# Multi-query attention with a residual: the first two batches' weights transposed by TensorE, and the last output products cut in two

## The chip, the core and the metric

The kernel runs on one core of a Trainium2 chip. A core has a matrix engine (TensorE, PE in the profile), three engines for elementwise work (VectorE, DVE; ScalarE, ACT; GpSimd, POOL), a sync engine (SP) whose queue issues most DMAs here, and 16 DMA engines. The engines run side by side and wait for each other by semaphores; each works through its own list of instructions in the order in which the program names them. PE, ACT and DVE reach PSUM, where products land; all reach SBUF.

The metric is the device time of one execution in microseconds (us). The times before are the median of three runs; one further execution was profiled.

## The reference, cut to what matters

x has 64 batches of 128 tokens with 512 features. There are 16 query heads of 64 and one head for keys and values, with a null key and a null value.

```python
xn = layernorm(x, g_in)
q = (xn @ Wq) * scale                      # 16 heads of 64
k, v = split(xn @ Wkv)                     # one head, null key/value in front
sim = einsum('bhid,bjd->bhij', q, k) + bias
sim = where(causal, -max, sim); sim = where(mask, sim, -max)
attn = softmax(sim)
out = einsum('bhij,bjd->bhid', attn, v)    # -> (b, n, 1024)
return x + layernorm(out @ Wo, g_out)
```

## The kernel before

The order of all instructions is written out by hand in `step(n)`, n from -6 to 62, and a few lines after the loop. Each step serves several batches at different stages: it normalizes and transposes tokens some ten batches ahead, makes the q products of four batches at a time (`product`, a Strassen-like scheme with seven products, whose sums are kept by `keep` and joined by `q_out`), makes scores of batch n + 2, the softmax of batch n + 1, the values of batch n and the output of batches before it. Near the end the distances grow by one: from B3 = 58 on, the softmax runs on `eb` = n + 2 and the scores on `nb` = n + 3. B is 64.

A batch passes these stages:

- **Bias** (POOL): `bias_add` (line 466) writes bias plus mask into the score tile S, `null_copy` (475) adds the null columns. S tiles come from a pool of two (tag "s"), so the bias of a batch has to wait until the tile of the batch two before has been read. One batch, B3 + 1 = 59, has its tile in the room of the transposed tokens (tag "xT").
- **Scores** (PE, line 495), in two halves: half 0 is the queries 0 to 63 against the first 64 keys, half 1 the queries 64 to 127 against all. `scores_add` (DVE, 508) adds them into S, `scores_max` (DVE, 513) takes the row maxima.
- **Exps** (ACT, 522), 8 rows of heads for each half, then `rinv` (DVE, 539) and `scale` (POOL, 543).
- **Transpose of the weights**: `blocks_T` (DVE, 575) transposes S in blocks of 32x32 into sb, and `blocks_move` (601) brings these blocks to their places in aTb with 14 DMAs on the queue of SP. With `take`, half of the 14 are issued by ACT; this is done for the first and the last batch. aTb exists once, from batch 56 on twice.
- **Values** (PE, 610): `values` starts the products of aTb with the values, `values_end` finishes and lets ACT move the result to oT (654). Where it is split, a small copy named done (DVE, 642) stands between the two.
- **Output**. Batches 1 to 58 go in pairs through `out_product` (719), `out_keep`, `out_part`, `pair_stats`, `pair_pow`, `pair_norm` (ACT, 765), `pair_residual` (DVE, 769 and 770). Batches 0 and 59 to 63 are "plain": `out_mm` (669) multiplies the eight chunks of oT with wo, followed by `out_stats` (DVE, 774 to 781, with a small pow on POOL), `residual` (ACT 795, POOL 796) and `store`. The first four chunks of oT come from the first of the two evacuations at line 654, the last four from the second.

PSUM rooms: ps_s (tag "s") holds one score half at a time, ps_w has two rooms, ps_q "a" and "c", ps_y "X" and "Y". Loads of x for the residual (`load_res`, 126) have two rooms, so the load of one batch waits on SP's queue until the residual of two before is done, and what is behind it on that queue waits too.

For the first batches: `blocks_T(0)` comes at the end of step -1 with seven of its DMAs on SP, and the other seven are issued by ACT in step 0, between the keep of a q product and the norm; `blocks_T(1)` comes in step 0 and its 14 DMAs on SP, ahead of `tokens_in(2)` (295), the transposed tokens of the third group of batches.

Of the kernel before, what the change touches and what calls it, by code (L numbers as in the profile page):

```python
# [8 lines left out]
FP = mybir.dt.float32  # L9
# [8 lines left out]
def kernel(  # L18
# [440 lines left out]

    def bias_add(b):  # L460
        g, t = divmod(b, GB)
        if b == B3 + 1:
            S[b] = gp.tile([P, R8, ROW], FP, tag="xT", name=f"s_{b}")
        else:
            S[b] = sp.tile([P, R8, ROW], FP, tag="s", name=f"s_{b}")
        nc.gpsimd.tensor_tensor(  # L466
            S[b][:, :, 1 : ROW - 1],
            biasp,
            mneg[g][:, t].unsqueeze(1).broadcast_to([P, R8, NL + N]),
            ALU.add,  # L470
        )
# [109 lines left out]
    def blocks_move(b, take=None):  # L581
# [3 lines left out]
        for u in range(2):  # L585
            for i in range(2):
                src = slice((2 * u + i) * Q, (2 * u + i + 1) * Q)
                for j in range(3 + i):
# [14 lines left out]
                        in_=sb[src, js].rearrange("p s e q -> p s (e q)"),  # L603
                    )

    pos = {}

    def value_mm(b, u, half, keys, vals, slots, start=True):
# [51 lines left out]
                bias=nv2,  # L660
            )

    def out_mm(b):
        pool, tag = ps_w, "w"
        if b > P_LAST:
            pool, tag = (ps_q, "c") if b == P_LAST + 2 else (ps_y, "XY"[b % 2])
        py = pool.tile([P, DIM], FP, tag=tag, name=f"py_{b}")
        for c in range(NC):
            nc.tensor.matmul(  # L669
                py, oT[b][:, c, :], wo[:, c, :], start=(c == 0), stop=(c == NC - 1)  # L670
            )
        ys[b] = py


    HE = DIM // 2
# [79 lines left out]
    def pair_pow(b):  # L755
        nc.gpsimd.tensor_tensor(yn[b][1], yn[b][1], nhalf, ALU.pow)

    def pair_norm(b):
        mv, rstd = yn.pop(b)
        nmr = small.tile([P, 1], FP, tag="nmro", name=f"nmro_{b}")  # L760
        nc.vector.tensor_scalar(nmr, mv[:, 0:1], rstd, -1.0, ALU.mult, ALU.mult)  # L761


        yn[b] = ps_y.tile([P, DIM], FP, tag="Y", name=f"yn_{b}")
        nc.scalar.activation(yn[b], ys[b], AF.Identity, bias=nmr, scale=rstd)
# [74 lines left out]
    def step(n):  # L840
        def ok(b, end=B):
            return 0 <= b < end
# [28 lines left out]
        if second:  # L871
            if n != B3 + 1:
                out_sums(p5673)
        elif ok(nb) and n >= 0:
            bias_add(nb)
            null_copy(nb)
        if third:
# [16 lines left out]
        if third:  # L894
            out_product(p4, 4, ps_y, "X", start=False)
        if one:
            out_mm(n - 1)
            if n == 1:
                out_stats(0)
        if fast:  # L900
            if f == 0:
                q_tile(qg)
            if n % 2:
                product(qg, f, 2, ps_w, "w")
        if last:
            product(last_g, last_f, 4, ps_q, "a", start=False)
        if soft:
# [144 lines left out]
        if n == B3:  # L1052
            out_sums(p12)
            scores(nb, 0)
            scores_add(nb, 0)
            pair_norm(p4 + 1)
            pair_residual(p4 + 1)
            store(p4 + 1)
            scores_max(nb, 0)
# [6 lines left out]
                scores_max(nb, 1)  # L1066
        if ok(n) and split:
            values_end(n, split)
        if eb == B - 1:
            blocks_move(eb, take=0)  # L1070
            blocks_move(eb, take=1)
# [43 lines left out]
        if ok(mk) and not ok(mkv):  # L1115
            kT_out(mk, k_T(mk))
        if n == -1:
            blocks_T(0)
            blocks_move(0, take=0)
        if n == B3 - 2:  # L1120
            bias_add(B3 + 1)
            null_copy(B3 + 1)
            scores(B3 + 1, 0)
            scores_add(B3 + 1, 0)
            scores_max(B3 + 1, 0)
        if 0 <= n < 4:
            out_weight_sum(n)
        if n == B2 - 2:
# [106 lines left out]
```

## Time and profile before

| what | before |
|---|---|
| time, median of 3 runs (lowest to highest) | 1135.81 us (1134.92 to 1136.13) |
| profiled execution, its time | 1134.49 us |
| its span, first to last instruction | 1132.7 us |
| mean granted TensorE clock | 0.995 |
| DMA, mean | 116 GB/s |

The span is what the profile shows; the execution's own time is 1.8 us longer. In timelines each row begins with its start and its length in us, both from the span's start, followed by engine, line, operation, output and inputs, the shapes, the count, and in brackets the idle time of the engine before it with the instruction that ended it. Matmuls of fp32 appear as two records each. Steps can be found in the timeline by their lines: step 0 is near 79 to 99 us, step 1 near 99 to 120; step 57 begins near 1030, step 58 near 1048, step 59 near 1063, step 60 near 1076, step 61 near 1090.

### The profile page before, as it was taken

The numbers are of one execution on the slowest core, as the hardware profiler recorded it, in microseconds if no ns is written. First come the engines' busy times: TensorE is split into PE (matmuls) and PEld (weight loads), VectorE is DVE, ScalarE is ACT, GpSimd is POOL, SyncE is SP. The second block draws the span as 40 slices with busy tenths as digits, with TensorE's granted clock in tenths as the row PEclk, the third lists the DMA queues.
The fourth block names the chain that finished last, engine by engine and source line by source line (L and its number), as shares of the span: only waits on it lengthen the run. The fifth ranks groups of instructions, "written<-read, shape, count | busy, mean of one in ns | idle before, by whom it ended". The sixth has DMA issues, their size and how long they took to land.

```text
span 1132.7 us, 27381 instructions
## 1 busy us (share of the span) xinstructions
PE 1084.5 (96%) x9700; PEld 869.1 (77%) x9700; DVE 807.5 (71%) x1737; ACT 678.5 (60%) x2710; POOL 745.9 (66%) x588
## 2 busy tenths in 40 slices
PE   6877999999999999999999999999999999999897
PEld 4454788888878888888888888888888888887642
DVE  6563677776787777788777778877777886666762
ACT  2344656566756656675666667666666755657661
POOL 5444877767665676857577686757767675676742
PEclk9998999999999999999999999999999999999999
DMA  6314234353453435335353533534353353422333
GB/s 184 123 37 126 73 123 118 93 167 100 126 127 120 115 98 163 103 125 135 104 135 97 164 106 122 136 116 121 97 164 107 120 136 112 103 73 72 95 97 107
DMA packets 109591, 131.39 MB, mean 116 GB/s; under 512 B 29712, under 2 KB 74256, under 8 KB 107664
## 3 DMA queue, kind: packets, MB, share of 16 engines
q1 hardware_dynamic: 107776, 127.95, 40.3%
q10 hardware_dynamic: 1680, 1.71, 0.5%
q8 instruction: 77, 1.26, 0.5%
q14 instruction: 58, 0.48, 0.1%
HBM read 54.86 MB, written 31.46 MB: 76 GB/s over the span
## 4 chain that ended last, share of the span: by engine, by line
PE 71%; POOL 7%; DVE 6%; DMA 6%; SPq 4%; issue 2%; ACT 2%; ACTq 1%; POOLq 0%; DVEq 0%
PE pa L422 15%; PE pyX L719 14%; PE pc L422 7%; PE ps L495 7%; PE pyY L719 7%; PE po L610 7%; PE pk L308 4%; PE pw L422 4%; PE pyw L719 3%; DMA x<-in_x_dram 3%; SPq L601 3%; PE py L669 2%; POOL s L466 2%; POOL xS L404 1%; POOL s L543 1%
## 5 line engine op out<-in xcount | busy, mean ns | idle before, releaser
L522 ACT ACTIVATE s<-s,nmax 128x65 f32<-128x65 f32 (+1 forms) x1024 | 372.1, 368 | 1.3 <-DVE nmax L513 0.9
L466 POOL TENSOR_TENSOR s<-biasp,mneg 128x1536 f32<-128x1536 f32 x64 | 221.1, 3455 | 108.3 <-DVE sb L575 105.1
L543 POOL TENSOR_TENSOR s<-s,rinv 128x512 f32<-128x512 f32 (+1 forms) x128 | 189.4, 1481 | 125.7 <-DVE nmro L761 88.6
L654 ACT ACTIVATE oT<-po,nv 128x512 f32<-128x512 f32 x128 | 81.1, 684 | 210.9 <-PE po L610 210.9
L522 ACT ACTIVATION_READ_ACCUMULATOR s<-s,nmax 128x1 f32 x1024 | 194.7, 190 | 0.0
L719 PE MATMUL pyX<-wT,oT 128*128 128x256 f32 x696 | 164.6, 379 | 1.1 <-DVE kyu L731 1.1
L719 PEld LDWEIGHTS pyX<-wT,oT 128*128 128x128 f32 x696 | 132.0, 190 | 19.8 <-DVE kyu L731 1.5
L508 DVE TENSOR_TENSOR s<-ps,s 128x512 f32<-128x512 f32 (+1 forms) x128 | 121.4, 949 | 14.8 <-PE ps L495 12.7
L495 PEld LDWEIGHTS ps<-kT,qT 64*64 64x64 f32 x4096 | 93.9, 135 | 46.9 <-DVE s L508 24.5
L422 PE MATMUL pa<-xS,wq 128*128 128x256 f32 x480 | 123.6, 380 | 2.5 <-ACT ku L433 1.5
L513 DVE TENSOR_REDUCE nmax<-s 128x8 f32<-128x520 f32 (+1 forms) x128 | 120.1, 938 | 5.1 <-POOL s L475 3.7
L575 DVE STREAM_TRANSPOSE sb<-s 128x1536 f32<-128x1536 f32 x64 | 113.5, 1773 | 11.8 <-POOL s L543 4.9
L495 PE MATMUL ps<-kT,qT 64*64 64x64 f32 (+1 forms) x4096 | 118.4, 252 | 3.7 <-DVE s L508 2.5
L610 PE MATMUL po<-aTb,vs 64*64 64x256 f32 (+1 forms) x1240 | 116.7, 383 | 1.3 <-DMA aTb<-sb 1.3
L433 ACT COPY ku<-pa 128x256 f32<-128x256 f32 x120 | 44.8, 373 | 93.1 <-PE pa L422 93.1
L422 PEld LDWEIGHTS pa<-xS,wq 128*128 128x128 f32 x480 | 86.8, 190 | 13.1 <-ACT ku L433 2.5
L422 PE MATMUL pc<-xS,wS 128*128 128x256 f32 x240 | 63.3, 386 | 8.3 <-POOL xS L404 7.3
L308 PE MATMUL pk<-wkv,xT 128*128 128x144 f32 x488 | 69.9, 286 | 0.0
L443 DVE TENSOR_TENSOR qT<-pw,kp 128x256 f32<-128x256 f32 x60 | 25.4, 423 | 59.9 <-ACT kp L433 59.8
L422 PE MATMUL pa<-xS,wS 128*128 128x256 f32 x240 | 68.0, 406 | 0.0
L610 PEld LDWEIGHTS po<-aTb,vs 64*64 64x64 f32 (+1 forms) x1240 | 57.5, 135 | 10.9 <-issue 4.6
L308 PEld LDWEIGHTS pk<-wkv,xT 128*128 128x128 f32 x488 | 63.4, 191 | 0.2
(114 smaller groups left out, 2060.7 us busy)
## 6 DMA issues: line engine op xcount, KB each, us to landing
aTb<-sb SPq DMA_DIRECT2D x378, 64.0 KB
x<-in_x_dram SPq DMA_DIRECT2D x64, 256.0 KB
res<-in_x_dram SPq DMA_DIRECT2D x64, 256.0 KB
out_dram<-y SPq DMA_DIRECT2D x64, 256.0 KB
aTb<-sb SPq DMA_DIRECT2D x504, 32.0 KB
xd<-xb SPq DMA_DIRECT2D x14, 1024.0 KB
xT<-xd SPq DMA_DIRECT2D x56, 256.0 KB
wo<-in_L_cond_Wo_dram SPq DMA_DIRECT2D x1, 2048.0 KB
```

What stands on the lines that cost most here:

```text
L308: nc.tensor.matmul(pkv, xT[g][:, t, kc, :], wkv[:, kc, :], start=(kc == 0), stop=(kc == KC - 1),)
L422: nc.tensor.matmul(prod[tag], w[:, kc, f * P : (f + 1) * P], t[:, :, kc, :], start=(start and kc == 0), stop=(kc == HK - 1), skip_group_ch ...
L466: nc.gpsimd.tensor_tensor(S[b][:, :, 1 : ROW - 1], biasp, mneg[g][:, t].unsqueeze(1).broadcast_to([P, R8, NL + N]), ALU.add,)
L495: nc.tensor.matmul(pv[u * DH : (u + 1) * DH, r, f, :], qT[g][rows, f, t, hf, u], kT[b][rows, 0:nk], start=True, stop=True,)
L508: nc.vector.tensor_tensor(sv, pss.pop((b, hf)), sv, ALU.add)
L513: nc.vector.tensor_reduce(nmax[b][:, hf], S[b][:, :, WITH_NULL[hf]], AX.X, ALU.max, negate=True)
L522: nc.scalar.activation(row, row, AF.Exp, bias=nmax[b][:, hf, k : k + 1], accum_out=rsum[b][:, hf, k : k + 1],)
L543: nc.gpsimd.tensor_tensor(sv, sv, rinvs.pop((b, hf)).unsqueeze(2).broadcast_to([P, R8, sv.shape[2]]), ALU.mult,)
L575: nc.vector.transpose(sb.rearrange("p j e q -> p e j q"), S[b][:, :, 1 : ROW - 1].rearrange("p e (j k) -> p e j k", k=Q),)
L610: nc.tensor.matmul(pos[b][u][r * DH : (r + 1) * DH, half], vals[keys, b % GB, 0:DH], aT_of(b)[keys, slots, r * NF : (r + 1) * NF], start=s ...
L654: nc.scalar.activation(oT[b][:, u * NF : (u + 1) * NF, :].rearrange("p f (s q) -> p s f q", q=Q), po[u].rearrange("p h i f q -> p (h i) f q"),
L719: nc.tensor.matmul(prod[key], h[:, c, :], w[:, c, :], start=(start and c == 0), stop=(c == HC - 1), skip_group_check=not start,)
```

## The change

For batches 0 and 1 the DVE transpose and the 14 DMAs are replaced by `attn_T_pe`: eight PE transposes of 128x128 for the upper keys, sixteen 64x64 products with parts of the identity for the lower keys, and three DVE copies into aTb. The group of batch 0 stands at the end of step -1, where `blocks_T(0)` stood; that of batch 1 stands in step 1, behind `out_mm(0)`, and `bias_add(3)` follows it.

Near the end:

- `out_mm` of batches 59 and more is cut in two: chunks 0 to 3 before the values of the next batch and chunks 4 to 7 behind them; that of batch 59 is cut around the values of batch 60, and so on. `out_stats` moves behind the second half.
- The bias of batch 62 (B3 + 4) goes into the room of the transposed tokens, and is made in step 58 instead of step 59. Batch 63 thereby takes the S tile that was batch 62's.
- `scores(59, 0)` with its add and maximum moves from the end of step 56 into step 57, behind the second product.
- `rinv` and `scale` of batch 61's first half move behind the keep of yu2 in step 59.
- The small DVE instruction nmr of batch 56 is split from `pair_norm` and comes before the values of step 58.

```diff
     def bias_add(b):
-        if b == B3 + 1:
+        if b in (B3 + 1, B3 + 4):
             S[b] = gp.tile([P, R8, ROW], FP, tag="xT", name=f"s_{b}")
...
+    def attn_T_pe(b):
+        pu = ps_s.tile([P, 2, NF, N], FP, tag="s", name=f"paU_{b}")
+        for k in range(R8):
+            nc.tensor.transpose(pu[:, k // NF, k % NF, :], S[b][:, k, UK], ident)
+        pl = ps_y.tile([P, R8, DH], FP, tag="X", name=f"paL_{b}")
+        for k in range(R8):
+            for u in range(2):
+                rows = slice(u * DH, (u + 1) * DH)
+                nc.tensor.matmul(pl[rows, k, :], S[b][rows, k, LK],
+                                 ident[rows, rows], start=True, stop=True)
+        for r in range(2):
+            nc.vector.tensor_copy(
+                aTb[:, 2:, r * NF : (r + 1) * NF, :].rearrange("p s f q -> p f s q"),
+                pu[:, r].rearrange("p f (s q) -> p f s q", q=Q),
+            )
+        nc.vector.tensor_copy(
+            aTb[:, 0:2].rearrange("p s e q -> p e s q"),
+            pl.rearrange("p e (s q) -> p e s q", q=Q),
+        )
...
-    def out_mm(b):
+    def out_mm(b, lo=0, hi=NC):
+        if lo == 0:
...
+            ys[b] = py
+        for c in range(lo, hi):
             nc.tensor.matmul(ys[b], oT[b][:, c, :], wo[:, c, :],
                              start=(c == 0), stop=(c == NC - 1))
...
-        elif ok(nb) and n >= 0:
+        elif ok(nb) and n >= 0 and n != 1:
             bias_add(nb)
             null_copy(nb)
...
         if one:
-            out_mm(n - 1)
+            out_mm(n - 1, 0, NF if n > B3 + 1 else NC)
             if n == 1:
+                attn_T_pe(1)
+                bias_add(nb)
+                null_copy(nb)
                 out_stats(0)
...
+        if n == B3 - 1:
+            scores(B3 + 1, 0)
+            scores_add(B3 + 1, 0)
+            scores_max(B3 + 1, 0)
...
         if soft:
             exps(eb, 0, 4)
+        if soft and n != B3 + 1:
             rinv(eb, 0)
             scale(eb, 0)
...
+        if n == B3:
+            bias_add(B3 + 4)
+            null_copy(B3 + 4)
...
-            if n == 0:
-                blocks_move(0, take=1)
...
         if n == B3 + 1:
+            rinv(eb, 0)
+            scale(eb, 0)
             blocks_T(n + 1)
             blocks_move(n + 1)
-            bias_add(nb)
-            null_copy(nb)
...
+        if n == B3:
+            pair_nmr(p4 + 1)
         if ok(n):
             values(n, split)
...
-        if one and n > 1:
-            out_stats(n - 1)
-        if n == 0:
-            blocks_T(1)
...
             values_end(n, split)
+            if n > B3 + 1:
+                out_mm(n - 1, NF)
...
+        if one and n > 1:
+            out_stats(n - 1)
...
         if n == -1:
-            blocks_T(0)
-            blocks_move(0, take=0)
+            attn_T_pe(0)
         if n == B3 - 2:
             bias_add(B3 + 1)
             null_copy(B3 + 1)
-            scores(B3 + 1, 0)
-            scores_add(B3 + 1, 0)
-            scores_max(B3 + 1, 0)
...
-    out_mm(B - 2)
+    out_mm(B - 2, 0, NF)
     values(B - 1, False)
     values_end(B - 1, False)
+    out_mm(B - 2, NF)
```

More of the change, by code (lines that the diff above doesn't have):

```diff
@@ L604, in blocks_move @@
                     )
+    def attn_T_pe(b):
[6 more added lines that the diff above has]
+                rows = slice(u * DH, (u + 1) * DH)
+                nc.tensor.matmul(
+                    pl[rows, k, :],
+                    S[b][rows, k, LK],
+                    ident[rows, rows],
+                    start=True,
+                    stop=True,
+                )
[7 more added lines that the diff above has]
+            pl.rearrange("p e (s q) -> p e s q", q=Q),
+        )
     pos = {}
@@ L661, in values_end @@
             )
-    def out_mm(b):
[L664 to L668, printed above, removed]
-            nc.tensor.matmul(
-                py, oT[b][:, c, :], wo[:, c, :], start=(c == 0), stop=(c == NC - 1)
+    def out_mm(b, lo=0, hi=NC):
+        if lo == 0:
+            pool, tag = ps_w, "w"
+            if b > P_LAST:
+                pool, tag = (ps_q, "c") if b == P_LAST + 2 else (ps_y, "XY"[b % 2])
+            py = pool.tile([P, DIM], FP, tag=tag, name=f"py_{b}")
+            ys[b] = py
+        for c in range(lo, hi):
+            nc.tensor.matmul(
+                ys[b],
+                oT[b][:, c, :],
+                wo[:, c, :],
+                start=(c == 0),
+                stop=(c == NC - 1),
             )
-        ys[b] = py
     HE = DIM // 2
@@ L756, in pair_pow, with pair_nmr @@
         nc.gpsimd.tensor_tensor(yn[b][1], yn[b][1], nhalf, ALU.pow)
-    def pair_norm(b):
+    nmrs = {}
+    def pair_nmr(b):
         mv, rstd = yn.pop(b)
@@ L761, in pair_norm @@
         nc.vector.tensor_scalar(nmr, mv[:, 0:1], rstd, -1.0, ALU.mult, ALU.mult)
+        nmrs[b] = nmr, rstd
+    def pair_norm(b):
+        if b not in nmrs:
+            pair_nmr(b)
+        nmr, rstd = nmrs.pop(b)
         yn[b] = ps_y.tile([P, DIM], FP, tag="Y", name=f"yn_{b}")
@@ L1068, in step @@
             values_end(n, split)
+            if n > B3 + 1:
+                out_mm(n - 1, NF)
+        if one and n > 1:
+            out_stats(n - 1)
         if eb == B - 1:
```

## The prediction

> **What bounds the kernel now.** I read the page first, then TensorE's order of time where its busy digits fall, then the other engines there.
>
> ```profile
> PE 1084.5 (96%) x9700; PEld 869.1 (77%) x9700; DVE 807.5 (71%) x1737; ACT 678.5 (60%) x2710; POOL 745.9 (66%) x588
> ...
> PE   6877999999999999999999999999999999999897
> ...
> PEclk9998999999999999999999999999999999999999
> ```
>
> TensorE (PE) sets the time: slices of 28.3 us are full from the fifth to the 37th. Only 0 to 113 us and 1020 us onward can give anything, and added PE work costs its full length. In the timeline of the first stretch (start, length, ..., idle time before and its releaser):
>
> ```profile
> 84.77 0.69 PE L495 MATMUL ps<-kT,qT 64*64 64x64 f32 x32
> 86.79 0.65 PE L610 MATMUL po<-aTb,vs 64*64 64x256 f32 x4 [1.33 <-DMA aTb<-sb]
> 91.84 0.69 PE L610 MATMUL po<-aTb,nv 64*64 64x256 f32 x2 [4.39 <-DMA aTb<-sb]
> ...
> 113.44 0.43 PE L610 MATMUL po<-aTb,nv 64*64 64x256 f32 x2 [1.64 <-DVE qT L443]
> ```
>
> Values(0) waits 5.7 us for the moved blocks of batch 0; values(1) waits 1.6 us for a q copy that stands behind exps on ACT. ACT itself is held:
>
> ```profile
> 83.14 4.83 ACTq L601 DMA_DIRECT2D aTb<-sb  x7
> ...
> 88.02 0.81 ACT L259 ACTIVATE x<-x,nmr,rstd 128x512 f32<-128x512 f32 x1 [4.53 <-DMA aTb<-sb]
> ```
>
> Seven of batch 0's DMAs are issued by ACT, in front of its second half of exps of batch 1. The table by windows (after the busy times: granted clock, DMA share, GB/s) shows what idle time costs besides:
>
> ```profile
> 92.00:97.00 5.00, 5.00 (x54) 3.76 (x54) 3.31 (x5) 0.59 (x2) 4.76 (x3) 0.53 0.01 3
> ...
> 113.40:117.50 4.10, 4.06 (x53) 2.83 (x53) 2.57 (x5) 1.74 (x4) 3.47 (x3) 0.58 0.26 74
> ```
>
> After both waits PE runs at about half clock. At the end the SP queue, POOL and DVE count:
>
> ```profile
> 1070.70 10.24 SPq L601 DMA_DIRECT2D aTb<-sb  x14
> 1080.99 4.93 SPq L126 DMA_DIRECT2D res<-in_x_dram  x2
> 1086.02 9.93 SPq L601 DMA_DIRECT2D aTb<-sb  x14
> ...
> 1097.69 13.74 SPq L601 DMA_DIRECT2D aTb<-sb  x21
> ```
> ```profile
> 1070.72 3.46 POOL L466 TENSOR_TENSOR s<-biasp,mneg 128x1536 f32<-128x1536 f32 x1 [0.88 <-DVE sb L575]
> ...
> 1108.27 0.65 PE L610 MATMUL po<-aTb,nv 64*64 64x256 f32 x4 [0.35 <-DMA aTb<-sb]
> ```
>
> From 1070 us SP issues almost without pause, 0.65 us a DMA; the bias of batch 62 keeps POOL from a scale; PE meets the last landing of batch 62 with 0.35 us to spare.
>
> **Part 1: two batches on TensorE.** Removed: 28 DMAs (21 on SP, 7 on ACT) and two DVE transposes of 1.77 us. Added per batch: 8 transposes, 16 small matmuls, 3 DVE copies.
>
> Transposes: in row L268 four take 0.60 us and one 0.27, so each further one 0.11; eight take 0.27 + 7 x 0.11 = 1.04. The Trainium skill, page "TensorE: Matmul & The Clock Gate", section "Part 4: PE-mode transpose", prices one at some 275 ns, mostly access latency; taken as serial that is 2.2 us for eight, 2.3 us more over both batches. The trace has the same 273 ns, but overlapped, so I take 1.04. The small matmuls have no row. Nearest is L495, 64x64x64, 16 matmuls (32 records) in 0.69 us on all four quadrants; these use the two diagonal ones, so between 0.7 and twice 0.69 = 1.4; I take 1.0. Sum 2.0 us a batch. A copy from PSUM with 128x512 elements is near L508's 0.69 us, three 2.1: DVE pays 0.3 us more than its transpose.
>
> Batch 0: S[0] is scaled at 76.96 + 1.91 = 78.9 on POOL; PE ends step -1's products at 77.9. It idles 1.0, works to 80.9, and the product begun at 78.54 slips 2.4. Behind it ACT's copy moves from 79.71 to 82.1; eight exps (2.65) and the keep bring ACT to 85.2. There its 4.83 us of DMA issue are gone: the norm follows once DVE's nmr is there (85.7), and exps(1,1), 8 x 0.39 = 3.1, end at 89.6, before 91.85. The copies end at 82.6; values(0) starts after scores(2,0) at 85.9. What is late next is values_end(0): its copy named done stands behind rinv(1,1) on DVE, which waits for those exps until 89.7. It ends at 90.5, before 96.3: -5.8. bias_add(2), which waited for DVE's transpose until 82.3, now waits for PE until 80.9 and ends at 84.5; scores(2,0) needs it at 86.
>
> Batch 1: its group stands behind out_mm(0). From 90.5: products 3.1, out_mm 7.0, the group 1.9 (S[1] is ready at 91.8); the product of 106.28 starts at 102.4: -3.9. bias_add(3) moves behind it and ends near 106; behind it on POOL wait the small pow of out_stats and scale(2,0), wanted at 106.6; first user of the bias is the add of 113.95 - 3.9 = 110.0, so it is covered by 4 us. tokens_in(2), on SP behind 14 DMAs, goes out some 9 us earlier; PE does not wait for it.
>
> The new wait before values_end(0) is 2.0 us (87.9 to 89.9). The same page, section "Why this matters for your kernels", allows idle gaps up to about 3 us without a clock loss: by it the start keeps -3.9. The row at 113.44 contradicts it: 1.64 us idle behind the same scores and values, then about 3.4 us at half clock, 1.7 lost. A 1.93 us gap before 59.77 cost no clock (granted 1.00). The likest row is the first, so I charge 1.7: **start -2.2**, between -0.7 (a long stretch like 89.95 to 96.4, 3.2 lost) and -5.6 (neither half-clock stretch of the old trace recurs).
>
> **Part 2: the end.** scores(59,0) moves behind product 2 of step 57: the 0.63 us wait at 1030.20 for DVE goes, the bias of 59 is long there: -0.6, carried on by a full PE. nmr(56) moves ahead of scores_add(61,0), which pays 0.08: yn(56) starts after ACT's evacuation instead of 0.72 later. kyu no longer waits behind rinv(61,0) (1068.22); PE waited 1.07 for it. Together exps(61,1) end at 70.0 (from here 1000 + x) instead of 71.3.
>
> bias_add(62) (3.46 + 0.21) goes to step 58, into POOL's idle 4.04 us before 1059.51, in the room of xT 15 whose last product ran at 1051. Cover left: 0.4 us; without it scale(60,0) slips. Now scale(61,1) starts at 70.1 instead of 74.4 and blocks_T(61) at 72.1 instead of 76.3. The 1.1 us wait before scores(62,1) goes. Softmax(62), then residual(57), end at 81.0 instead of 85.5: SP's second load of x stands for residual(57), so blocks_move(61) begins at 81.6 instead of 86.0, and blocks_move(62) at 93.2 instead of 97.7. Its last landing comes at 103.8 instead of 1108.2.
>
> So SP, not PE, sets the pace: PE waits near 80, 92 and 102, each 1.6 to 2.0 us. The halves of out_mm fill those gaps and the 0.8, 1.0 and 0.7 us for oT; they move PE work and take none away. After 103.8 PE has values(62) 1.5, half of out_mm(61) 3.5, out_mm(62) 7.0, values(63) 1.3 and out_mm(63) 7.0: 124.1, before 126.9: **end -2.8**. ACT's seven DMAs for batch 63 end near 107.0, the evacuation of 62 follows at 107.8; PE wants it at 108.8. out_stats behind values_end costs DVE nothing; its waiter, ACT's residual, stands before exps(63) and comes at 91.1, before 93.1. The tail of 5.8 us stays. Bounds of the end: 0 (SP's pace stays) to -4.4.
>
> **Sum.** -2.2 - 2.8 = -5.0 of the profiled execution's 1134.49 (span 1132.7 and 1.8 around): 1129.5. The median of runs, 1135.81, lies 1.3 higher; by it 1130.8. I write 1130.2, between them.
>
> **Rivals.** (a) Clock kept: the earlier values(0) keeps PE dense and neither half-clock stretch returns: -5.6 - 2.8, 1126 to 1127.5. For: the old drop followed 4.39 us idle; against: the 2.0 us wait stays. Chance 0.20. (b) The end gives nothing: landings, not issue, hold values(61) and (62), with 14 DMAs each as before: only -2.2, 1133. For: the 0.35 us of 1108.27; against: the 4.93 us in the SP rows is a wait for DVE. 0.13. (c) The transposes don't free values(0): ACT's later exps hold values_end(0) near 94 and the start is even: -2.8, 1132.4. For: ACT slips 2.4; against: 4.83 us leave its queue. 0.08. (d) Slower: PE's half clock at the new SP waits. If values(61) and (62) each start a 6.4 us stretch as at 89.95, each costs 3.2; with the long one at the start, -0.7 - 2.8 + 6.4 = +2.9, 1138. It decides from two such stretches on. Against: a wait beside full 128x128 products (59.77) cost no clock. 0.07. My forecast has 0.52.
>
> **Numbers.** Less than 0.2% (2.3 us) can't be told from no change. Faster: 0.52 + 0.20 + half of (b) + most of (c), 0.84; slower 0.07; same 0.09. The forecast's own range is 1128 to 1132.5; (a) and (b) widen it to 1126.3 and 1133.6.
>
> **What will show it.** No DMA to aTb before 100 us; values(0) without a DMA wait, values_end(0) near 90.5 behind DVE rinv; the clock column for 90 to 94; product 2 of step 1 between 102.4 and 104. POOL's bias of 62 before 1060; blocks_move(61) near 1082 - start gain; DMA waits of PE before values(60), (61), (62). I am wrong if the group takes over 3 us a batch, if values_end(0) stays after 94, or if SP's pace at the end is unchanged.

## The result, and the profile after

| what | before | after |
|---|---|---|
| median of 4 runs each on one chip | 1135.97 us (1134.92 to 1136.99) | 1129.25 us (1128.47 to 1131.23) |
| ratio, 95% interval | | 0.9944 (0.9926 to 0.9961) |
| the same two kernels on another chip (e5), 17 and 6 runs | 1136.10 us | 1130.89 us, 0.9951 (0.9936 to 0.9965) |
| profiled execution, its time and span | 1134.49, 1132.7 us | 1131.23, 1129.4 us |

The kernel is faster by 0.5 to 0.6%, some 6 us. The execution that was profiled was the slowest of the four, 2 us above their median, so the traces have to account for 3.3 us of span only.

The lines of the changed kernel are shifted: values are at 636 (610 before), the copy named done at 668 (642), the evacuation to oT at 680 (654), `out_mm` at 697 (669); the transposes are 610 and 615, their copies 623 and 627. The page of the changed kernel:

```profile
PE 1089.5 (96%) x9780; PEld 873.0 (77%) x9780; DVE 808.0 (72%) x1741; ACT 678.1 (60%) x2710; POOL 745.3 (66%) x588
...
PE   6988999999999999999999999999999999999987
```

PE has 80 records more (2 x 40), and its second to fourth slices are each a tenth fuller. PE's order of time where batch 0 is transposed (start, length, work, and in brackets the idle time before it and its releaser):

```profile
79.81 1.09 PE L610 MATMUL paU<-ident,s 128*128 128x128 f32 x8 [0.90 <-POOL s L543]
80.83 1.15 PE L615 MATMUL paL<-ident,s 64*64 64x64 f32 x32
81.91 1.13 PE L422 MATMUL pa<-xS,wq 128*128 128x256 f32 x4
...
87.93 1.10 PE L495 MATMUL ps<-kT,qT 64*64 64x128 f32 x32
91.20 0.96 PE L636 MATMUL po<-aTb,vs 64*64 64x256 f32 x8 [2.17 <-DVE done L668]
92.10 2.07 PE L422 MATMUL pa<-xS,wS 128*128 128x256 f32 x4
...
112.53 0.43 PE L636 MATMUL po<-aTb,nv 64*64 64x256 f32 x2 [1.64 <-DVE qT L443]
```

The 5.7 us of DMA waits are gone. In their place stand one wait of 2.17 us, for done, and 0.90 us before the transposes, which wait for the scaled weights. The 1.64 us wait of values(1) is unchanged. DVE shows whom done stood behind:

```profile
90.92 0.20 DVE L539 RECIPROCAL rinv<-rsum 128x8 f32<-128x8 f32 x1 [3.05 <-ACT s L522]
91.04 0.10 DVE L668 COPY done<-po 128x1 f32<-128x1 f32 x1
```

Three stretches of the changed kernel, by windows (after the busy times: granted clock, which is 1.00 at full speed, DMA share, GB/s):

```profile
91.00:95.00 4.00, 3.79 (x17) 2.65 (x18) 3.11 (x5) 1.64 (x3) 3.79 (x2) 0.57 1.00 221
113.00:117.00 4.00, 3.84 (x59) 2.78 (x54) 2.76 (x6) 2.95 (x5) 3.88 (x3) 1.00 0.00 0
1081.00:1085.00 4.00, 3.68 (x42) 2.60 (x43) 3.72 (x6) 1.32 (x3) 1.57 (x1) 0.57 0.44 121
```

There is half clock behind the new wait, none behind the wait of values(1), where the old kernel had it, and a new stretch near the end. PE's waits there, and SP's queue:

```profile
1060.33 1.97 PE L750 MATMUL pyY<-wT,yS 128*128 128x256 f32 x8 [0.47 <-DVE y L809]
...
1064.56 1.99 PE L750 MATMUL pyX<-wT,oT 128*128 128x256 f32 x8 [0.52 <-DVE kyu L762]
...
1078.58 0.43 PE L636 MATMUL po<-aTb,nv 64*64 64x256 f32 x2 [0.92 <-DMA aTb<-sb]
...
1081.32 1.98 PE L495 MATMUL ps<-kT,qT 64*64 64x128 f32 x32 [1.66 <-DVE s L508]
...
1097.06 3.70 PE L697 MATMUL py<-wo,oT 128*128 128x512 f32 x8 [0.31 <-ACT oT L680]
...
1102.14 0.65 PE L636 MATMUL po<-aTb,nv 64*64 64x256 f32 x4 [0.80 <-DMA aTb<-sb]
...
1108.04 3.70 PE L697 MATMUL py<-wo,oT 128*128 128x512 f32 x8 [0.61 <-ACT oT L680]
```
```profile
1067.15 9.89 SPq L601 DMA_DIRECT2D aTb<-sb  x14
1077.09 2.74 SPq L126 DMA_DIRECT2D res<-in_x_dram  x2
1079.92 9.91 SPq L601 DMA_DIRECT2D aTb<-sb  x14
...
1091.58 15.74 SPq L601 DMA_DIRECT2D aTb<-sb  x21
```

SP's wait for the residual has shrunk from 4.93 us to 2.74. From 1060 us on PE waits 5.3 us (the seven waits above), where the old kernel waited 7.2 from 1063 on (1.18, 1.07, 1.10, 0.56, 0.81, 1.03, 0.35, 0.68, 0.42); the 0.63 us at 1030 is gone too. That is 2.5 us less idle time, of which the half clock at 1081 takes 1.7 back: 4 us at a mean of 0.57 hold 3.4 us at half clock, and half of that is lost.

**Where the time went.** Landmarks on PE, read from the timelines, for all runs. L0 is the start of the last product of step -1 (77.78 in the changed kernel); the next columns are times after L0, of the product behind values_end(0), of product 2 of step 1, and of scores(4, 0). The last product of step 56 divides middle from end; the end reaches to the last output product. The last column lists half clock up to PE's last product. us throughout.

| run | L0 | values_end(0) over | product 2 | scores(4, 0) | middle | end | half clock (us) |
|---|---|---|---|---|---|---|---|
| before | 76.89 | 19.41 | 29.39 | 53.35 | 898.30 | 98.37 | 89-96, 113-117 |
| after | 77.78 | 14.32 | 27.49 | 51.16 | 897.45 | 97.46 | 43-47, 91-94, 1081-1084 |
| e5, after once more | 78.16 | 14.50 | 27.44 | 51.10 | 897.92 | 96.27 | 91-94, 1081-1084 |
| e1, first part alone | 78.21 | 14.02 | 25.86 | 49.51 | 898.34 | 97.87 | 43-46 |
| e2, second part alone | 76.87 | 19.21 | 28.99 | 52.56 | 899.64 | 98.60 | 89-95, 1106-1109 |
| e3, work in the new wait | 76.69 | 14.02 | 25.85 | 49.95 | 900.26 | 98.48 | 110-113, 1103-1107 |
| e4, rinv(1, 1) later | 75.66 | 11.62 | 24.67 | 49.09 | 897.92 | 100.83 | 109-112, 1054-1061, 1082-1085 |
| e12, e4 once more | 78.87 | 11.62 | 24.67 | 49.09 | 898.82 | 97.37 | 44-47, 112-115, 1081-1085 |
| e9, e4 and a product earlier | 76.84 | 11.62 | 24.67 | 48.47 | 897.53 | 97.46 | 1078-1082 |
| e10, e4 with one batch on PE | 76.61 | 11.62 | 22.62 | 49.70 | 898.04 | 97.15 | 106-110, 124-127, 1079-1083 |
| e6, work in waits of the end | 76.82 | 14.02 | 25.86 | 49.92 | 897.66 | 97.31 | 110-113 |
| e7, output not cut | 78.53 | 14.03 | 25.86 | 49.53 | 897.31 | 98.55 | 43-46, 1094-1101 |
| e8, bias 62 where it was | 78.74 | 14.44 | 27.48 | 51.16 | 896.14 | 100.85 | 44-47, 61-64, 92-95, 1082-1088 |
| e11, e4 and an earlier end | 77.44 | 11.62 | 24.67 | 48.97 | 897.15 | 96.91 | 110-113, 1093-1096 |

In the profiled pair: load stage +0.9, start -2.2, middle -0.85, end -0.9, and -0.25 behind PE's last product: -3.3. L0 and the middle vary by up to 3 and 4 us between profiles of kernels that do the same work there, so a single span says little about 2 us. That is why the verdicts below rest on medians for the time and on landmarks for the place.

### The profile page after: what moved, and what is told of

It reads as the page before. It is cut to its first block, busy times and chain, and to the rows that moved or that the text cites. A ratio compares the mean times of both kernels' runs of the same rounds, so it can differ in the third digit from the quotient of the medians.

```text
span 1129.4 us, 27505 instructions
## 1 busy us (share of the span) xinstructions
PE 1089.5 (96%) x9780; PEld 873.0 (77%) x9780; DVE 808.0 (72%) x1741; ACT 678.1 (60%) x2710; POOL 745.3 (66%) x588
## 3 DMA queue, kind: packets, MB, share of 16 engines
q8 instruction: 78, 1.28, 0.5%
q10 hardware_dynamic: 1248, 1.38, 0.4%
## 4 chain that ended last, share of the span: by engine, by line
PE 68%; DMA 8%; POOL 7%; DVE 6%; SPq 5%; issue 3%; ACT 3%; POOLq 0%; ACTq 0%; DVEq 0%
PE pa L422 14%; PE pyX L750 13%; PE pc L422 7%; PE ps L495 7%; PE po L636 6%; PE pyY L750 6%; DMA x<-in_x_dram 6%; PE pk L308 4%; SPq L601 4%; PE pw L422 3%; PE pyw L750 3%; PE py L697 3%; ACT s L522 2%; POOL s L543 1%; POOL xS L404 1%
## 5 line engine op out<-in xcount | busy, mean ns | idle before, releaser
L575 DVE STREAM_TRANSPOSE sb<-s 128x1536 f32<-128x1536 f32 x62 | 110.0, 1774 | 11.6 <-POOL s L543 4.6
L636 PE MATMUL po<-aTb,vs 64*64 64x256 f32 (+1 forms) x1240 | 114.2, 380 | 2.2 <-DVE done L668 2.2
L246 POOL TENSOR_TENSOR rstd<-rstd,nhalf 128x1 f32<-128x1 f32 x64 | 35.8, 559 | 44.5 <-DVE rstd L245 44.4
```

The source lines that it names most:

```text
L575: nc.vector.transpose(sb.rearrange("p j e q -> p e j q"), S[b][:, :, 1 : ROW - 1].rearrange("p e (j k) -> p e j k", k=Q),)
L636: nc.tensor.matmul(pos[b][u][r * DH : (r + 1) * DH, half], vals[keys, b % GB, 0:DH], aT_of(b)[keys, slots, r * NF : (r + 1) * NF], start=s ...
```

## The experiments

Each was timed in five rounds beside the kernel before. Diffs are against the changed kernel and cut to what matters.

### The two parts apart

**e1**, the first part alone: everything from the old kernel but `attn_T_pe`, its two calls and the moved bias_add(3).

> Only the first two batches' transposes go to TensorE; the end is as before. If the start is worth what the prediction charged, the time falls by 2.2 us (up to 3.9 where the clock holds behind the wait before values_end(0)), and from the product that starts at 76.89 us in the old trace to scores(4,0) the stretch shrinks from 53.35 to about 51.2 us. If the change's whole gain comes from the end, the time is that of before within 1 us.

**e2**, the second part alone: batches 0 and 1 go through `blocks_T` and `blocks_move` again.

> Only the edits of the end; the first batches are moved by DMA as before. If SP's pace sets the end and its queue shifts with residual(57), the time falls by 2.8 us, from 98.4 us between the last product of step 56 and the last output matmul's end to about 95.6. If landings hold the end as before, by under 1 us. In either case the sum of this gain and that of the start alone should be the change's 6.7 us within the noise, since a full TensorE carries both.

Measured: e1 1130.89 us, ratio 0.9956 (0.9940 to 0.9972); e2 1133.73 us, 0.9977 (0.9962 to 0.9992). Of 1135.8 us that is 5.0 (3.2 to 6.8) for the first part and 2.6 (0.9 to 4.3) for the second. Together they make 7.6, beside 6.4 and 5.6 for the whole change: the parts add up within their intervals, and by the medians the first is the larger, the reverse of the forecast (the two intervals overlap). In e1 PE's order of time has the same wait as the changed kernel and no half clock behind it:

```profile
91.64 0.66 PE L636 MATMUL po<-aTb,vs 64*64 64x256 f32 x8 [2.17 <-DVE done L668]
92.23 1.13 PE L422 MATMUL pa<-xS,wS 128*128 128x256 f32 x4
```

The eight values take 0.66 us instead of 0.96, the product 1.13 instead of 2.07. Its windows there, and at a half-clock stretch of the load stage:

```profile
91.60:95.00 3.40, 3.36 (x25) 2.70 (x26) 2.95 (x3) 1.53 (x3) 3.36 (x2) 1.00 0.97 222
43.00:47.00 4.00, 4.00 (x21) 3.93 (x19) 0.44 (x2) 1.49 (x3) 4.00 (x2) 0.57 0.10 30
```

So scores(4, 0) comes 3.8 us earlier than before, not 2.2. The 2.17 us wait alone does not decide the clock. Nor is less idle time the larger part of this gain: from L0 to product 2, PE idles 3.07 us in e1 and 7.42 before, 4.35 less, but works some 3.3 us more. The rest of the 3.5 us gained there is clock: the old kernel lost 2.45 us in the half-clock stretch from 89.9 to 96.7 (4.89 us of work at half speed), and e1 has none there.

In e2 the end was no shorter than before (98.60): PE waited 1.71 us for done and 1.73 for a DMA, and lost clock at 1106; its median still shows a gain.

### The clock behind the new wait

**e3**: nine products of the identity with itself, whose results nobody reads, fill the wait.

```diff
+        if n == 0:
+            fill_pe(9)          # before values_end(0)
```

> The changed kernel with nine extra 128x128 identity matmuls on TensorE (about 2 us, results unused) in the wait before values_end(0). If that wait's cost is its own 2.2 us and also some 1.7 us of half clock behind it, the filler keeps the clock at 1.00 from 91 to 96 us and product 2 of step 1 comes some 1.7 us earlier after the start of step -1's last product (25.8 instead of 27.5 us), the time falls by up to 1.7. If the half clock has nothing to do with idle time, or the clock in other runs held anyway, no change or a loss of some tenths.

PE's order of time and the clock there:

```profile
87.88 2.27 PE L1192 MATMUL fill<-ident 128*128 128x128 f32 x18
90.12 0.66 PE L636 MATMUL po<-aTb,vs 64*64 64x256 f32 x8
```
```profile
92.00:94.00 2.00, 2.00 (x13) 1.72 (x12) 1.05 (x1) 0.49 (x3) 2.00 (x2) 1.00 1.08 222
```

The clock holds, and product 2 stands at 25.85, where e1 has it without any filling: the half clock costs 1.6 us of the start (27.49 less 25.85). But in this run the 3.4 us at half clock came at 110, behind values(1), and scores(4, 0) gained 1.2 us only. The time is 1130.65 us, 0.9958 (0.9942 to 0.9974), that of the unfilled kernel. Filling one wait does not pay here.

**Which wait costs clock.** The traces answer more of this than the runs compared above. Where a window of 1 us holds the start of a half-clock stretch, its mean clock tells where the stretch starts: a mean of 0.74 is 0.52 us at half clock. In e8:

```profile
44.00:45.00 1.00, 1.00 (x8) 0.86 (x6) 0.00 (x0) 0.99 (x3) 1.00 (x1) 0.74 0.00 0
61.00:62.00 1.00, 0.66 (x2) 0.57 (x3) 0.00 (x0) 0.30 (x1) 0.92 (x2) 0.77 0.34 90
92.00:93.00 1.00, 0.83 (x8) 0.26 (x8) 1.00 (x4) 0.00 (x0) 0.83 (x1) 0.63 0.77 221
1082.00:1083.00 1.00, 0.00 (x0) 0.00 (x0) 0.44 (x3) 0.59 (x5) 0.16 (x1) 0.57 0.32 68
```

The four stretches start at 44.48, 61.54, 92.26 and 1082.14 us. These distances are 5, 9 and 290 times 3.413 us. In each of the fourteen profiles all stretches start on one such grid, within 0.01 us, and it lies differently against the program from one execution to the next. Cut along it, the 2.17 us wait is no longer one case. In after, e5 and e8, 2.11 to 2.17 us of it fall into one interval of the grid (88.02 to 91.44 in after), and half clock follows. In e1, e6 and e7 a boundary divides the wait, no interval holds more than 1.64 us of it (e1: 1.34 before 90.81, 0.83 behind), and none follows. Over all profiles, from 30 to 1124 us, half clock followed each of the 20 full-clock intervals in which PE, by its matmul records, idled 2.0 us or more, none of the 4,352 with less than 1.3 us, and 13 of the 65 between. What decides between 1.3 and 2.0 us stays open.

**e4**: `rinv(1, 1)` and `scale(1, 1)` go behind the adds and maxima of batch 2, just ahead of `values_end(0)`, so that done no longer stands behind ACT's exps on DVE. **e12** is the same kernel once more on another chip.

```diff
-            if ok(n + 1) and fill:            # behind scores_add(nb, 0)
+            if n < 0 and ok(n + 1):
                 rinv(n + 1, 1)
                 scale(n + 1, 1)
...
+        if n == 0:                            # before values_end(0)
+            rinv(1, 1)
+            scale(1, 1)
```

> The changed kernel with rinv(1,1) and scale(1,1) behind the adds and maxima of batch 2 on DVE. If the wait before values_end(0) is only DVE's small copy standing behind rinv(1,1), values_end(0) comes right after scores(2,1), near 89 us, and a wait of about 1 us for ACT's evacuation takes its place; product 2 of step 1 comes 2 to 3 us earlier than in the changed kernel. If ACT's exps hold everything anyway, the wait moves to the next product and nothing is gained.

> The kernel of e4 once more, to tell whether its 8 us are real. If its start is worth 1 to 2 us over the changed kernel, the ratio to the kernel before lies near 0.993 again and the stretch to scores(4,0) near 49 us, with no half clock before 96 us; if e4 was a lucky draw of the clock, the ratio is 0.9945 to 0.995, as for the changed kernel.

Measured: e4 1126.93 us, 0.9929 (0.9910 to 0.9948); e12 1128.30 us, 0.9929 (0.9914 to 0.9944). Both ratios lie below those of the changed kernel, by 1.5 and 2.2 thousandths, so this is the fastest version of the study. The intervals of each single pair overlap, but the 12 runs of e4 and e12 average 1128.1 us and the ten of the changed kernel (after, e5) 1130.3, a gain of 2.2 us (0.8 to 3.6). The order of time on PE in e4:

```profile
86.74 0.61 PE L636 MATMUL po<-aTb,vs 64*64 64x256 f32 x8
...
89.41 0.33 PE L342 MATMUL pk<-ident,ktok 128*128 128x128 f32 x1 [0.99 <-ACT oT L680]
```

values_end(0) no longer waits. 0.99 us comes back one product later, since the key transposes need the PSUM room that ACT empties. Product 2 is 2.8 us earlier than in the profile of the changed kernel, of which 1.2 is the wait and 1.6 the clock, and so 1.2 earlier than in e1, where the clock held.

**e9** goes on from e4: the wait of values(1) is for a q copy behind ACT's exps, so product 1 of step 1 with its `keep` and `q_out` goes ahead of them.

```diff
+        if n == 1:                            # before exps(eb, 1, 0, 2)
+            product(qg, f, 1, ps_q, "a")
+            keep("a", "p1")
+            q_out(qg, f, lo_t, "w", "p1")
...
-        if fast:                              # where it stood
+        if fast and n != 1:
             product(qg, f, 1, ps_q, "a")
```

> The kernel of e4 with product 1 of step 1, its keep and its q_out ahead of the second half of exps. If the 1.64 us wait of values(1) is only ACT's keep standing behind six exps, it goes, no half clock follows it, and the stretch to scores(4,0) falls from e4's 49.1 us to about 47; the time falls by 1 to 2 us against e4. If values(1) then waits for ACT's exps of batch 2 by way of DVE, the wait comes back one step later and nothing is gained.

Measured: 1129.98 us, 0.9952 (0.9935 to 0.9969), no gain over e4. PE's order of time says why:

```profile
106.97 0.61 PE L636 MATMUL po<-aTb,vs 64*64 64x256 f32 x8
110.16 1.10 PE L495 MATMUL ps<-kT,qT 64*64 64x128 f32 x32 [2.57 <-DVE done L668]
```

values(1) runs without a wait, and the next scores wait 2.57 us for DVE in its stead. Of 1.64 us removed, 0.6 arrives at scores(4, 0), and part of that may be the half clock at 109, which the profile of e4 has and that of e9 has not.

### Is it worth transposing batch 1 on PE?

**e10** is e4 with batch 0 alone on PE; batch 1 takes the DVE transpose and 14 DMAs on SP.

```diff
-        elif ok(nb) and n >= 0 and n != 1:
+        elif ok(nb) and n >= 0:
...
-                attn_T_pe(1)
-                bias_add(nb)
-                null_copy(nb)
...
+            blocks_T(1)                       # behind scale(1, 1)
```

> The kernel of e4 with only batch 0 on TensorE; batch 1 goes by DVE's transpose and 14 DMAs on SP again. In the old trace values(1) waited for no DMA, so batch 1's group would only cost its 2.1 us of PE: product 2 of step 1 comes 2.1 us earlier (22.6 us after step -1's last product instead of 24.7). The blocks can land near 105 us and values(1) wants them near 105.5: if they are in time the time falls by some 2 us against e4; if not, values(1) waits for DMA by 1 to 3 us and the gain is given back.

Measured: 1132.51 us, 0.9969 (0.9958 to 0.9981), against 0.9929 for e4. Batch 1's group costs PE 2.05 us (product 2 at 22.62 without it, 24.67 with it), and values(1) waits 1.63 us for qT in both: its blocks come in time by DMA. That leaving the group out loses more than it saves is shown by the ratios, whose intervals are apart. The timelines of e10 show a way for it, from SP's queue to POOL and then to PE:

```profile
94.39 9.20 SPq L601 DMA_DIRECT2D aTb<-sb  x14
103.64 2.02 SPq L295 DMA_DIRECT2D xT<-xd  x4
105.70 0.43 SPq L126 DMA_DIRECT2D res<-in_x_dram  x1
```
```profile
113.59 1.27 POOL L835 TENSOR_TENSOR y<-y,res 128x512 f32<-128x512 f32 x1 [4.71 <-DMA res<-in_x_dram]
```
```profile
124.31 2.07 PE L422 MATMUL pc<-xS,wS 128*128 128x256 f32 x4 [3.14 <-POOL xS L404]
```

The load for residual(0) goes out behind the 14 DMAs and `tokens_in(2)`, at 105.70 instead of 91.30 in the changed kernel. POOL stands 4.71 us at that residual, and the token sums behind it hold PE for 3.14 us, with half clock behind (124 to 127). This profile accounts for a part only. It is of the fastest of e10's eight runs (1129.08 us), and at scores(4, 0) it has lost 0.6 us against e4 (49.70 and 49.09), while the medians differ by some 4.5. The granted clock of the runs differs too, with a mean of 0.993 in e10 and of 0.9965 and 0.996 in e4 and e12. That makes some 3.5 us of lost clock (an estimate, 0.003 to 0.0035 of 1130 us), most of which this profile does not place.

### The end

**e5** is the changed kernel again, on the chip of e6 to e8, as their measure.

> The changed kernel once more, unaltered, with a trace of its own. If the half-clock stretches belong to the free-running state of the clock and not to the program, they lie at other places than in its first trace (91 to 95 us and 1081 to 1085 us) or are missing at one of them, and the stretch from step -1's last product to scores(4,0) is either 51.2 us again or 49.5. The median stays within 1.5 us of 1129.25.

Measured: 1130.89 us, 0.9951 (0.9936 to 0.9965). Two of the three half-clock stretches are the same, that of the load stage is gone; the end is 96.27, 2.1 shorter than before, where the first profile had 0.9. So two profiles of one kernel differ by 1.2 us in the end. That the two stretches recur is no sign that they belong to the program: the grids of the two executions happen to lie within 0.1 us of each other (91.44 and 91.53).

**e6**: work whose results nobody reads in the waits before scores(63, 1) and before values(62).

```diff
+            if n == B3 + 4:
+                fill_pe(5)                    # before values(n, split)
...
+        if n == B3 + 2:
+            fill_pe(7)                        # before scores(nb, 1)
```

> The changed kernel with idle PE filled at two places of the end by identity matmuls whose results are unused: seven before scores(63,1), five before values(62). If half clock behind these waits gives back the end's gain, no window of the end below 0.99 is left there, the end (from the last product of step 56 to the end of the last output matmul) takes 96 to 96.5 us instead of 97.5, and the time falls by about 1 us. If the clock is not what costs, the end stays at 97.5 or grows by what the fillers add, at most 2.6.

Measured: 1129.59 us, 0.9944 (0.9929 to 0.9958). No half clock is left in the end up to the last output product, yet it takes 97.31 us, since the 3.1 us of filling (1.83 and 1.28) take the place of waits and of the loss. In time it can't be told from e5; inconclusive.

**e7**: `out_mm` in one piece again, ahead of the next values.

```diff
-            out_mm(n - 1, 0, NF if n > B3 + 1 else NC)
+            out_mm(n - 1)
...
-            if n > B3 + 1:
-                out_mm(n - 1, NF)
```

> The changed kernel with the plain outputs whole, in front of the next values. If the halves only fill what PE would wait anyway, SP still sets the pace, values(61) and values(62) come at the same landings, and the waits for oT return (0.8, 1.0 and 0.7 us in the old trace), at most 2.5 us slower. If the halves do nothing because the landing of the blocks holds the end, the time is the same.

Measured: 1130.75 us, 0.9949 (0.9937 to 0.9961): the same as e5. PE waits for ACT's evacuation again, 0.81 us at 1082.81, 0.42 at 1107.63, and between them:

```profile
1095.60 10.01 PE L697 MATMUL py<-wo,oT 128*128 128x512 f32 x16 [4.05 <-ACT oT L680]
```

The waits move and collect in one of 4.05 us, with half clock from 1094 to 1101 (10.01 instead of 7.13 for the product). The medians are the same. Cutting the output products in two gives nothing that these runs can measure.

**e8**: the bias of batch 62 back in step 59 and in the pool of two; the cuts stay.

```diff
-        if b in (B3 + 1, B3 + 4):
+        if b == B3 + 1:
...
-        if n == B3:
-            bias_add(B3 + 4)
-            null_copy(B3 + 4)
...
             blocks_T(n + 1)
             blocks_move(n + 1)
+            bias_add(nb)
+            null_copy(nb)
```

> The changed kernel with the bias of batch 62 back in step 59 and in the pool of two. If this move is what draws SP's queue forward, scale(61,1) starts some 3 to 4 us later, blocks_move(61) some 3 us later, and the time grows by 1.5 to 2.8 us, nearly the end's whole gain. If the end's gain comes from the halves, it changes by less than 1 us.

Measured: 1132.57 us, 0.9974 (0.9963 to 0.9985), 2.6 us more than e5 by the ratios. POOL, SP and PE in its timelines:

```profile
1066.81 3.45 POOL L466 TENSOR_TENSOR s<-biasp,mneg 128x1536 f32<-128x1536 f32 x1 [0.88 <-DVE sb L575]
...
1070.47 1.91 POOL L543 TENSOR_TENSOR s<-s,rinv 128x1024 f32<-128x1024 f32 x1
```
```profile
1076.47 5.53 SPq L126 DMA_DIRECT2D res<-in_x_dram  x2
```
```profile
1083.49 1.98 PE L495 MATMUL ps<-kT,qT 64*64 64x128 f32 x32 [3.75 <-DVE done L668]
```

The scale of batch 61 starts right behind the bias, SP waits 5.53 us for the residual, and PE 3.75 us. So the bias in another room carries the gain of the end: without it the gain is gone, without the cuts (e7) it stays. e8 keeps the other edits of the end (scores(59, 0), the rinv and scale of batch 61, nmr of 56) and is no faster than e1, which has none of them (0.9974 and 0.9956). What these three add beside the bias was not run alone. The intervals of e8 and e5 just touch, and e8's own profile also lost clock at 61 and 92, which its edit does not reach.

**e11**, on top of e4, takes the next wait of the SP queue away: the second load of x goes behind the blocks of batch 61, and scores(63, 0) with its add ahead of the last exps of batch 62.

```diff
-        if 0 <= n and plain(n):
+        if 0 <= n and plain(n) and n != B3 + 1:
...
+        if n == B3 + 1:                       # behind blocks_move(61)
+            load_res(n)
...
+        if n == B3 + 2:                       # before exps(eb, 1, 6)
+            scores(nb, 0)
+            scores_add(nb, 0)
...
-        if sc and n != B3:                    # where they stood
+        if sc and n not in (B3, B3 + 2):
             scores(nb, 0)
```

> The kernel of e4 with the residual load of batch 59 behind the blocks of batch 61 on SP's queue, and scores(63,0) with its add ahead of the second half of the softmax of 62. If SP's wait for residual(57) (2.7 us in the changed kernel) sets the end, blocks_move(61) starts 2 to 3 us earlier, the wait of 1.7 us or more before scores(63,1) goes, and the end is 1 to 2.5 us shorter than with the same clock in the changed kernel. If landings or ACT hold the end, no gain.

Measured: 1127.87 us, 0.9935 (0.9923 to 0.9947), like e4. SP's queue runs without a wait, and PE's next wait is ACT's:

```profile
1073.70 0.58 SPq L126 DMA_DIRECT2D res<-in_x_dram  x1
1074.39 9.25 SPq L601 DMA_DIRECT2D aTb<-sb  x14
```
```profile
1077.28 1.10 PE L495 MATMUL ps<-kT,qT 64*64 64x128 f32 x32 [1.00 <-DVE s L508]
...
1093.67 5.30 PE L697 MATMUL py<-wo,oT 128*128 128x512 f32 x8 [2.55 <-ACT oT L680]
```

Counted from the last product of step 56, blocks_move(61) starts 2.7 us earlier than in the changed kernel (50.8 against 53.5), and the end is 0.5 us shorter (96.91 against 97.46). The rest turned into a wait for the evacuation of batch 61 on ACT.

## Why the prediction was right, and where its sum was not

The total held: 1130.2 us predicted, 1129.25 and 1130.89 measured, and the sign with it. By parts it was -2.2 and -2.8; the runs give -5.0 (-6.8 to -3.2) and -2.6 (-4.3 to -0.9). One term was mis-sized, the clock at the start. That the total came so close is in part luck: the parts measured alone add up to 7.6 us, and the whole change gives 6.4 and 5.6 by its two ratios.

**The group on PE.** Predicted 2.0 us a batch: 1.04 for the transposes and 1.0 for the small products between ends of 0.7 and 1.4. Measured 2.10 from 79.81 to 81.91: eight transposes in 1.09, the 32 records on two quadrants in 1.15. e10's 2.05 confirms it by leaving one group out. The copies took 1.28 and 0.68 us on DVE, against 2.1 in all. The serial price, an estimate from the some 275 ns that the Trainium skill gives for a transpose in one kernel ("TensorE: Matmul & The Clock Gate", section "Part 4: PE-mode transpose"), would have been 2.2 us for the eight alone; the trace says half of that.

**values_end(0).** The mechanism was right to the releaser: done behind rinv(1, 1), behind ACT's exps. It was predicted 5.8 us earlier and came 5.1 earlier after L0; the wait was 2.17 us, predicted 2.0. Rival (c), that ACT's later exps hold it, falls: they began at 87.70 and ended near 90.9.

**The clock: the term that was mis-sized.** I charged 1.7 us for half clock behind the new wait, and nothing for the old stretch at 113. The charge was right (1.6 us measured) where the stretch came (product 2 at 27.49, 27.44 and 27.48 in the profiles of after, e5 and e8) and wrong where it did not (25.86 in e1, e6 and e7, 25.85 with the wait filled). The same 2.17 us wait had either outcome. So -2.2 and rival (a)'s first half, -3.9, were both near, each for some executions: scores(4, 0) came 2.2 us earlier in the first group and 3.8 in the second. The median of e1, 5.0 us, lies on the second side, and the forecast's -2.2 outside its interval. What it holds beyond 3.8 us is within the scatter. The granted clock, with a mean of 0.9977 over e1's seven runs and of 0.9934 over the 24 beside them, makes some 4.9 us less of lost clock (an estimate, 0.0043 of 1130 us), and the profiled execution of before, at 0.995, lost less than that mean.

I took the clock of a place for a property of the wait; it is a property of the execution too, by where its grid lies. The Trainium skill has the grid, on the page "TensorE: Matmul & The Clock Gate", section "What's actually happening": the gate judges activity by windows of 3413 ns that run freely, independent of the kernel. The traces agree, with the grid of 3.413 us shown above, and each stretch here is one such window long or two: 4 us at a mean clock of 0.57 are 3.44 us at half clock.

**The old stretch at 113.** It did not return in the profiles of after, e1, e5, e7 and e8, with the 1.64 us wait in place; in e3, e4, e6, e10, e11 and e12 one stood there. Rival (a) counted 1.7 us for its absence, and -5.6 in all. e1's profile has neither stretch and gained 3.8, so that size was wrong. e2, whose start is that of before, shows why: without the stretch, product 2 to scores(4, 0) takes 23.57 us, against 23.96 in before with it. Up to the product at 119.50 the stretch costs 1.3 us (13.22 from product 2, 11.93 in e2), but 0.9 of that comes back in waits that get shorter, the largest for POOL's token sums (before, then after):

```profile
129.18 1.13 PE L422 MATMUL pc<-xS,wS 128*128 128x256 f32 x4 [0.97 <-POOL xS L404]
...
127.88 1.13 PE L422 MATMUL pc<-xS,wS 128*128 128x256 f32 x4 [1.37 <-POOL xS L404]
```

**tokens_in(2).** "PE does not wait for it" was right of the tokens and wrong of the queue. They went out at 89.50 instead of 105.80, 16 us earlier and not 9, and with them the load for residual(0) (before, then after):

```profile
107.87 0.43 SPq L126 DMA_DIRECT2D res<-in_x_dram  x1
...
91.30 0.43 SPq L126 DMA_DIRECT2D res<-in_x_dram  x1
```

In e10's profile, where the load goes out late again, PE meets a 3.14 us wait and a half-clock stretch. The prediction valued the emptied queue at nothing. bias_add(3), predicted to end near 106, ran from 105.49 to 108.94. PE's wait for the token sums behind it on POOL, at 127.88, went from 0.97 to 1.37 us, but not by this move: e2, where bias_add(3) stands as before, has 1.38 us, and e4, where it is moved, 0.97. The longer wait goes with the missing half clock at 113.

**The end.** Steps up to SP's queue were right: counted from the last product of step 56, scale(61, 1) was predicted 4.3 us earlier and came 4.1 earlier (41.8 against 45.9), blocks_move(61) 4.4 and 4.0, blocks_move(62) 4.5 and 4.0. The bias of 62 ran on POOL from 1052.58 to 1056.03, with 0.35 us idle before scale(60, 0): the cover of 0.4 held. Three PE waits were predicted, near 80, 92 and 102, of 1.6 to 2.0 us each; measured are 0.92 and 1.66 us near 80, 0.31 at 97 and 0.80 at 102. What I did not list is whom the wait at 1081.32 is for: the add of scores(63, 0), which stood on DVE behind rinv(62, 1) and thus behind ACT's exps. It is the same pattern as done at the start:

```profile
1080.39 0.20 DVE L539 RECIPROCAL rinv<-rsum 128x8 f32<-128x8 f32 x1 [0.92 <-ACT s L522]
...
1080.59 0.68 DVE L508 TENSOR_TENSOR s<-ps,s 128x512 f32<-128x512 f32 x1
```

And "the evacuation of 62 follows at 107.8; PE wants it at 108.8" missed: ACT's seven DMAs took 6.03 us in front of it, 5.45 before, and PE waited 0.61 us for it. The size, -2.8, agrees with the 2.6 of e2; the profiles of after and e5 show 0.9 and 2.1. How much of the end's gain an execution keeps depends also on half clock, such as the 1.7 us at 1081: **rival (d)** happened with one short stretch where it needed two long ones. Rival (b), that the landings hold the end, falls with blocks_move(61) and with e8. That the halves "only fill gaps" was right: e7, without them, has the same time.

**What stays open.** What decides about half clock where PE idles between 1.3 and 2.0 us of one interval; most of e10's loss; and the gain of the end to better than 1 us, since stretches and scatter of that size come and go.

## What to carry to other kernels

When DMAs are taken off a shared queue, price the queue, not only the data: follow every instruction that stood behind them to its last waiter. Here the second batch's weights were never late, and in e10's profile it was the residual's load behind them that made PE wait. A small copy that another engine waits for should not stand in program order behind an instruction that waits for a third one; moving rinv a few places down was worth 2.2 us (0.8 to 3.6), nearly what the whole end gave. Beside a full engine, price a half-clock stretch as an outcome with a chance, look for a wait for another engine behind it that takes up part of the loss, and judge a gain of 2 us by medians, since two profiles of one kernel can differ by that.

## What the runs showed of the hardware

- Half clock comes in pieces of about 3.4 us, one or two in a row, that start on a grid of 3.413 us within each profile. A piece costs some 1.7 us of dense PE work, and less where a wait behind it takes it up (0.4 us net for the one at 113). Waits of 1.64 to 2.57 us had one behind them or none, in part as they fell on the grid: 1.64 us at 113.44 in the old kernel had one and at 112.53 in the changed kernel none; 2.17 us had one in three profiles (after, e5, e8) and none in three (e1, e6, e7). The same holds where nothing was changed: the wait of 2.24 us for ACT before 42.8 had one in the profile of e1 and none in that of before. The allowance of about 3 us in the Trainium skill, page "TensorE: Matmul & The Clock Gate", section "Why this matters for your kernels", did not hold here as a safe bound.
- Eight fp32 transposes of 128x128 in a row took 1.04 to 1.09 us. Sixteen 64x64 products on two diagonal quadrants took 1.15 us, where as many of the same size on all four take 0.69.
- ACT is held for as long as it issues DMAs: seven took 6.03 us (1100.56) and kept an evacuation of 0.6 us from PE.
- L0, the end of the load stage, moved between 75.7 and 78.9 us over the profiles, though no kernel changed anything ahead of it. In the five profiles with a half-clock stretch at 43 to 47 us it lay at 77.8 to 78.9, in the others at 75.7 to 78.2.
